# Norm sums, list indices and list masks: a PSUM operand for small VectorE operations in a four-layer graph-attention stack

## The chip, the cores and the metric

The kernel runs on one core of one Trainium2 chip. The metric is the device time of a whole execution in microseconds, as the median of several runs. Profiles come from one execution each; their times are counted from the first instruction. Engines are named as in the profile: PE (TensorE), PEld (its weight loads), DVE (VectorE), ACT (ScalarE), POOL (GpSimd), and SP (SyncE), which here only issues DMAs.

## The reference

The input x has 8 batches of 2048 rows of 64 features; adj is a 2048 x 2048 matrix of zeros and ones, with few ones outside its first rows. Four layers follow each other, each of the form x = x + f(relu(layernorm(x))):

```python
# layer 0: dot-product attention over the ones of adj
scores = einsum('bnd,bmd->bnm', h, h) * D ** -0.5
out = einsum('bnm,bmd->bnd', softmax(where(adj > 0, scores, -1e12)), h)
# layers 1 and 3: additive attention
h = h @ W
e = leaky_relu((h @ a1)[:, :, None] + (h @ a2)[:, None, :], 0.2)
out = elu_or_relu(softmax(where(adj > 0, e, -9e15)) @ h)
# layer 2: four dot-product heads over adj + I, a projection, one more
# dot-product attention, leaky_relu and a layernorm of the result
```

`_layernorm` subtracts the mean over the 64 features and divides by the root of the variance plus 1e-5.

## The kernel before

Since adj is sparse, the kernel turns it into lists and gathers rows by them. The 8 batches lie beside each other, so a row is 8 x 64 = 512 numbers (F = 512, B = 8), and the 2048 rows are 16 tiles of 128 partitions. For each tile, `lists` (from L620 on) multiplies a tile of adj by a falling key, takes the largest keys with MAX8 and MATCH_REPLACE8 on DVE (L632 to L644), and writes row numbers into `idx` (L652 for the first K entries of each row, L707 for the T packed ones, which hold the entries beyond K of the few long rows) and masks for padding into `mba` and `mbb` (L654, L708). `qidx` (L704) is the like for a query table. `ROWS`, `PACKED` and `WIDTH` set K, T and the number of keys for each tile; together the 16 tiles have 81 slots, and 26 gathered slots fit into SBUF at a time (`RING`).

Six stages follow each other in time, held apart by tables in DRAM that have to be complete before rows can be gathered from them:

1. norm of the input, 16 row tiles, into table 0, and the mean of all rows (L363, L375)
2. lists, gathers from table 0, scores, weighting, layer 0's result, its norm, table 1
3. additive attention of layer 1, its norm, table 2 and the query table
4. layer 2's four heads, table 3
5. layer 2's last attention, its own norm and the next layer's, table 4
6. additive attention of layer 3, output

Gathers (L259) are indirect DMAs, one for each slot, issued by POOL. POOL also weights rows (L389, L782), sums rows for the mean row (`acc`, L368) and takes the power -0.5 in the norms (L299). SP issues all other DMAs in a queue of its own: tiles of adj (L619), rows of x and of the tables (L268), stores of rows (L363), of x (L489) and of the mean row (L375).

The norm has two parts, written as stages of a software pipeline: `norm_a` sums a tile's rows (L276); then either it takes minus the mean (L288) and has ACT square x with that as a bias, eight times, one for each batch (L290), or it takes the mean (L280), subtracts it (L283) and has ACT square the difference (L284). `norm_b` sums the squares (L296), makes variance plus epsilon of it (L297), and POOL takes the power (L299) and, in the first form, multiplies by minus the mean (L301). `scaled` lets ACT apply it, in eight instructions again (L307). Stages 1 and 3 use the first form, 2 and 5 the second; stage 5 has two norms for each tile.

`tiny` hands out pieces of one PSUM tile of 128 x 512, `bank[0]`, in turn and from the start again when the end is reached. A new such tile is made for stages 1 and 2, for 3, and for 5 and 6. Before the change it holds the mean of L280, and copies of weights and scores that DVE reads (L541, L556, L880); all of these are written and read by DVE alone. The results of L276, L288, L296 and L297 lie in SBUF, and so do both operands of L652, L654, L707 and L708.

`pipeline` calls its stages for tile n, n-1, n-2 and so on in one step, the last stage first. The source order isn't the order of execution: when the program is built, a scheduler with cost estimates of its own writes each engine's queue, within the dependencies that it sees between tiles. Each engine then works through its queue in order. A change in the operands can therefore move instructions on all engines.

Of the kernel before, what the change touches and what calls it, by code (L numbers as in the profile page):

```python
# [8 lines left out]
F32 = mybir.dt.float32  # L9
# [4 lines left out]
OP = mybir.AluOpType  # L14
AX = mybir.AxisListType

P = 128
NEG = -1.0e30
SLOPE = 0.2
EPS = 1e-5  # L20
# [16 lines left out]
QE = 4  # L37

SPREAD = 3


MAKING = [15, 14, 13, 0, 12, 11, 10, 1, 9, 2, 8, 3, 7, 4, 6, 5]
# [19 lines left out]
def edge_stack(ctx: ExitStack, tc: tile.TileContext, x_in, adj, w1, w1t, a1, wh, wht, bh, wo, bo,  # L62
# [9 lines left out]
    nc = tc.nc  # L72
    N, F = x_in.shape
    D = gamma.shape[0]
    B = F // D
    NT = N // P
    H = bh.shape[0] // D
    INV_D = 1.0 / D
# [6 lines left out]
    small = ctx.enter_context(tc.tile_pool(name="small", bufs=4))  # L85
# [8 lines left out]
    idx = const.tile([P, NS], I32, name="idx")  # L94
    mba = const.tile([P, NS], F32, name="mba")
# [111 lines left out]
    def heads(t, n=B):  # L207
        return t.rearrange("p (b d) -> p b d", b=n)

    def wide(t, n=B):  # L210
        return t[:, :, None].to_broadcast([P, n, D])
# [15 lines left out]
    bank, spot, rows_pool, more_pool, own_pool, thin = [None], [0], [None], [None], [None], [None]  # L227
    kept = {}

    def tiny(n):  # L230

        at = spot[0] if spot[0] + n <= F else 0
        spot[0] = at + n
        return bank[0][:, at:at + n]

# [16 lines left out]
    def gather(k, i, st, behind=None):  # L252

        n = SLOTS[i]
        assert sum(SLOTS[j] for j in held) + n <= RING
        held[i], front[0] = front[0], (front[0] + n) % RING
        cols = table[k].shape[1]
        for t in range(n):
            g = nc.gpsimd.indirect_dma_start(  # L259
                out=ring[:, (held[i] + t) % RING, :cols], out_offset=None, in_=table[k][:, :],  # L260
                in_offset=bass.IndirectOffsetOnAxis(ap=idx[:, OFF[i] + t:OFF[i] + t + 1], axis=0))
            if behind is not None and t == 0:
                tc.add_manual_dep(g.ins, behind.ins.name, mybir.DependencyInfo(
                    mybir.DependencyClass.Sync, mybir.DependencyReason.DATA), reason="gather")
# [7 lines left out]

    def norm_a(src, st, centre):

        s = small.tile([P, B], F32, name="ln_s")
        nc.vector.tensor_reduce(s, heads(src), AX.X, OP.add)  # L276
        st["sq"] = rows_pool[0].tile([P, F], F32, name="ln_sq", bufs=4)
        if centre:
            mean = tiny(B)
            nc.vector.tensor_scalar(mean, s, INV_D, None, op0=OP.mult)  # L280
            st["less"] = None
            st["src"] = rows_pool[0].tile([P, F], F32, name="ln_xc", bufs=3)
            nc.vector.tensor_tensor(heads(st["src"]), heads(src), wide(mean), op=OP.subtract)  # L283
            nc.scalar.activation(st["sq"], st["src"], AF.Square)  # L284
            return
        st["src"] = src
        st["less"] = small.tile([P, B], F32, name="ln_m")
        nc.vector.tensor_scalar(st["less"], s, -INV_D, None, op0=OP.mult)  # L288
        for b in range(B):
            nc.scalar.activation(st["sq"][:, b * D:(b + 1) * D], src[:, b * D:(b + 1) * D], AF.Square,  # L290
                                 bias=st["less"][:, b:b + 1])

    def norm_b(st):

        q = small.tile([P, B], F32, name="ln_q")
        nc.vector.tensor_reduce(q, heads(st["sq"]), AX.X, OP.add)  # L296
        nc.vector.tensor_scalar(q, q, INV_D, EPS, op0=OP.mult, op1=OP.add)  # L297
        st["rstd"] = small.tile([P, 2, B], F32, name="ln_r")
        nc.gpsimd.tensor_tensor(st["rstd"][:, 0, :], q, mhalf, op=OP.pow)  # L299
        if st["less"] is not None:  # L300
            nc.gpsimd.tensor_tensor(st["rstd"][:, 1, :], st["less"], st["rstd"][:, 0, :], op=OP.mult)  # L301
# [17 lines left out]
    def pre_b(i, st):  # L319
        norm_b(st)  # L320
# [165 lines left out]
    def add_store(i, st, p, centre, more=0.0):  # L486
        x = st["x"]
        nc.vector.scalar_tensor_tensor(x, p, more, x, op0=OP.add, op1=OP.add)
        nc.sync.dma_start(out=xs[i], in_=x)  # L489
        norm_a(x, st, centre)  # L490
# [24 lines left out]
    def additive(k, wd, *finish):  # L515
        def take(i, st):
            n = order.index(i)
            gather(k, i, st, taken[k, order[n - SPREAD]] if n >= SPREAD else None)

# [14 lines left out]
        def first(i, st):  # L534
            K, T = ROWS[i], PACKED[i]
            w = slots(w_all, i)
            s = slots(s_all, i)
            n = 2 * B if k == 4 else B
            fs = f1s[:, i].rearrange("p t b -> p (t b)")[:, :n]
            pr = tiny(2 * B)  # L540
            nc.vector.tensor_copy(pr[:, :n], fs)  # L541
            pv = by_edge(i, fs, n)
            for t, m, g in rows(i, 0, K):
                nc.vector.tensor_tensor(s[:, t:t + m, :], g[:, :, F:], pr[:, None, :B].to_broadcast([P, m, B]),
                                        op=OP.add)
            for t, m, g in rows(i, K, K + T):
                nc.vector.tensor_tensor(s[:, t:t + m, :], g[:, :, F:], pv[:, t - K:t - K + m, :B], op=OP.add)
            taken[k, i] = leaky(s, s)
            if k == 4:
                nc.vector.tensor_tensor(s[:, :K, :], s[:, :K, :], pr[:, None, B:].to_broadcast([P, K, B]),  # L550
                                        op=OP.subtract)
                nc.vector.tensor_tensor(s[:, K:, :], s[:, K:, :], pv[:, :, B:], op=OP.subtract)
                nc.vector.tensor_scalar(s, s, 60.0, None, op0=OP.min)
            nc.scalar.activation(w, s, AF.Exp)  # L554
            wp = tiny((K + T) * B)
            nc.vector.tensor_copy(wp, w.rearrange("p t b -> p (t b)"))  # L556
            st["wp"] = wp.rearrange("p (t b) -> p t b", b=B)
# [31 lines left out]
    with tc.tile_pool(name="rows", bufs=2) as rp:  # L589
        rows_pool[0] = rp  # L590
        sel_all[0] = rp.tile([P, sum(PACKED) * P], F32, name="sel", bufs=1)
        with tc.tile_pool(name="lists", bufs=2) as pool, \
# [14 lines left out]
            pe = pool.tile([P, NT], F32, name="pe", bufs=1)  # L607
            nc.gpsimd.iota(pe, pattern=[[P, NT]], base=0, channel_multiplier=1,
                           allow_small_or_imprecise_dtypes=True)
            nn = pool.tile([P, NT], F32, name="nn", bufs=1)  # L610
            nc.vector.tensor_scalar(nn, pe, -1.0, N + 1.0, op0=OP.mult, op1=OP.add)
            tri = pool.tile([P, P], F32, name="tri", bufs=1)
# [8 lines left out]
            def lists(i, st):  # L621

                K, T, W = ROWS[i], PACKED[i], WIDTH[i]
# [15 lines left out]
                ell = small.tile([P, W + 2], F32, name=f"ell{W}", bufs=2)  # L639
# [9 lines left out]
                at = OFF[i]  # L649
                me = nn[:, i:i + 1]  # L650
                nc.scalar.copy(ell[:, W + 1:W + 2], me)
                nc.vector.tensor_scalar(idx[:, at:at + K], ell[:, :K], -1.0, N + 1.0, op0=OP.mult, op1=OP.add)  # L652
                if K > 1:
                    nc.vector.tensor_scalar(mba[:, at + 1:at + K], ell[:, 1:K], 0.0, NEG, op0=OP.is_equal, op1=OP.mult)  # L654
                st8 = small.tile([P, 8], F32, name="st8")
                deg, half, nmid = st8[:, 0:1], st8[:, 1:2], st8[:, 2:3]
                junk = small.tile([P, W], F32, name=f"junk{W}", bufs=1)
# [15 lines left out]
                for e0 in range(0, E, LS):  # L673
                    n = min(LS, E - e0)
# [5 lines left out]
                for t0 in range(0, T, 4):  # L680
                    n = min(4, T - t0)
# [5 lines left out]
                ke = small.tile([P, max(PACKED)], F32, name="ke")[:, :T]  # L687
                V = W - K
                step = min(T, F // (V + 2))
                mp = mbb[:, at + K:at + K + T]  # L690
                for t0 in range(0, T, step):
                    n = min(step, T - t0)
# [6 lines left out]
                    for t in range(n):  # L699
                        eq = pool.tile([P, P], F32, name="eq")  # L700
                        nc.vector.scalar_tensor_tensor(eq[:, :V], iotaj[:, :V], col[:, t:t + 1], pv[:, t, :V],
                                                       op0=OP.is_equal, op1=OP.mult,
                                                       accum_out=ke[:, t0 + t:t0 + t + 1])
                    nc.vector.tensor_scalar(qidx[:, POFF[i] + t0:POFF[i] + t0 + n], pv[:, :, V + 1], -1.0, N + 1.0,  # L704
                                            op0=OP.mult, op1=OP.add)
                    nc.vector.tensor_tensor(mp[:, t0:t0 + n], ke[:, t0:t0 + n], pv[:, :, V + 1], op=OP.is_equal)
                nc.vector.tensor_scalar(idx[:, at + K:at + K + T], ke, -1.0, N + 1.0, op0=OP.mult, op1=OP.add)  # L707
                nc.vector.tensor_scalar(mp, mp, NEG, None, op0=OP.mult)  # L708

            pipeline(xin_rows, lambda i, st: norm_a(st["x"], st, False), pre_b, pre_c(None), pre_d(0, None))  # L710
            pipeline(load_adj, lists, take0, both(first0, xin_rows), second, third0, pre_b, pre_c(u1),
                     pre_d(1, u1))

# [148 lines left out]
    with psum_pools()[0] as ps_q, psum_pools()[1] as ps_t, tc.tile_pool(name="rows2", bufs=2) as rp:  # L862
# [33 lines left out]
        def third3(i, st):  # L896
            y = st["y"]
            divide(st, y)
            nc.vector.tensor_tensor(heads(y), heads(y), over_d(bo_b), op=OP.add)
            t = rows_pool[0].tile([P, F], F32, name="z2", bufs=4)  # L900
            leaky_max(t, y, rows_pool[0].tile([P, F], F32, name="att"))
            norm_a(t, st, True)
# [28 lines left out]
        v = small.tile([P, 4], F32, name="v", bufs=1)  # L931
# [520 lines left out]
```

## Time and profile before

| | us |
|---|---|
| median of 3 runs | 1659.34 |
| lowest and highest | 1657.62, 1660.49 |
| span of the profiled execution | 1660.9 |
| DVE busy | 1311.9 |
| PE busy | 1214.6 |
| POOL busy | 1151.1 |
| ACT busy | 741.6 |

The profiled execution's time is given by its span alone; nothing around it is listed. Busy times of different engines overlap, so they don't add up to the span. What counts is which engine is full in which stage, and what ends each engine's waits there. A group of instructions is shown by its source line, engine and operation, what it writes and reads, the shapes, and how many there are.

### The profile page before, as it was taken

The page shows a single profiled execution, that of the slowest core. Times are in us where ns is not written, and L with a number is a line of the kernel's source. Part 1 is how long each engine was busy: PE and PEld are TensorE (multiplying, and loading weights), DVE is VectorE, ACT ScalarE, POOL GpSimd, SP SyncE. Part 2 cuts the span into 40 slices and gives each one's busy share as a digit, 9 for nine tenths or more (in the row PEclk, how much of TensorE's full clock was granted, in tenths as well). Part 3 has the DMA queues.
Part 4 walks back from the last instruction along what each step waited for, and adds up shares of the span by engine and source line. Part 5 has one row for each costly group of instructions (what it writes and reads, how often), then busy time and mean ns, then how long its engine had stood idle before and what let it go on. Part 6 is the DMA issues. An engine that isn't in the chain of part 4 may idle for free. (4 is left out here: it accounts for less than half of the span.)

```text
span 1660.9 us, 15702 instructions
## 1 busy us (share of the span) xinstructions
PE 1214.6 (73%) x3771; PEld 606.7 (37%) x3771; DVE 1311.9 (79%) x2674; ACT 741.6 (45%) x2362; POOL 1151.1 (69%) x903
## 2 busy tenths in 40 slices
PE   0025576776789974599997999999576868846898
PEld 0012243343454541234343344443233424423555
DVE  5978999994669987799999799861179979954667
ACT  5851223443257783356632455554334445560011
POOL 5765866786764215899689889998277889656650
PEclk9998877986889997799999999999877978857899
DMA  5545554453776537656255345300273443126771
GB/s 167 181 163 179 171 191 164 140 193 125 213 256 231 183 157 271 233 180 222 92 202 184 123 142 188 138 13 13 102 259 121 146 127 114 64 77 198 228 213 63
DMA packets 85787, 266.94 MB, mean 161 GB/s; under 512 B 14627, under 2 KB 14659, under 8 KB 75446
## 3 DMA queue, kind: packets, MB, share of 16 engines
q0 software_dynamic: 37328, 141.05, 27.4%
q1 hardware_dynamic: 48358, 124.79, 21.0%
q8 instruction: 32, 0.52, 0.1%
q14 instruction: 69, 0.57, 0.1%
HBM read 208.74 MB, written 57.05 MB: 160 GB/s over the span
## 5 line engine op out<-in xcount | busy, mean ns | idle before, releaser
L259 POOL DMA_INDIRECT g<-table,idx x405 | 396.2, 978 | 222.4 <-issue 131.7
L782 POOL TENSOR_TENSOR wh<-g,w 128x1024 f32<-128x1024 f32 x162 | 307.3, 1917 | 30.0 <-PE y L797 27.9
L394 PE MATMUL y<-wg,ident 128*128 128x512 f32 x392 | 232.4, 720 | 74.4 <-POOL wg L389 67.8
L299 POOL TENSOR_TENSOR ln_r<-ln_q,mhalf 128x8 f32<-128x8 f32 x80 | 135.9, 1702 | 129.0 <-DVE ln_q L297 93.0
L769 DVE TENSOR_REDUCE s<-prod 128x32 f32<-128x2048 f32 x81 | 183.9, 2285 | 14.6 <-ACT w L771 14.4
L389 POOL TENSOR_TENSOR wg<-g,w 128x1024 f32<-128x1024 f32 (+1 forms) x91 | 160.0, 1767 | 39.7 <-ACT w L445 31.7
L797 PE MATMUL y<-wh,ident 128*128 128x512 f32 x320 | 154.3, 609 | 28.1 <-POOL wh L795 24.4
L394 PE MATMUL y<-wg,selt 128*128 128x512 f32 x256 | 142.7, 669 | 6.0 <-POOL wg L389 6.0
L394 PEld LDWEIGHTS y<-wg,ident 128*128 128x128 f32 x392 | 79.6, 223 | 160.4 <-POOL wg L389 82.8
L797 PE MATMUL y<-wh,selt 128*128 128x512 f32 x256 | 124.6, 613 | 10.4 <-POOL wh L782 10.4
L805 ACT ACTIVATE yn<-y,rec 128x64 f32<-128x64 f32 x512 | 110.7, 366 | 27.6 <-PE y L797 26.8
L765 DVE TENSOR_TENSOR prod<-q,g 128x2048 f32<-128x2048 f32 x49 | 111.4, 2274 | 5.2 <-ACT g L763 5.1
L389 DVE TENSOR_TENSOR wg<-g,tiny 128x1024 f32<-128x1024 f32 (+1 forms) x92 | 98.1, 1086 | 12.3 <-PE y L394 11.9
L451 DVE SCALAR_TENSOR_TENSOR zt<-m,bhc,att 128x512 f32<-128x512 f32 x64 | 47.2, 737 | 74.9 <-ACT att L450 74.8
L408 PE MATMUL m<-w,selt 128*128 128x8 f32 (+1 forms) x384 | 61.0, 262 | 54.0 <-ACT w L554 19.1
L408 PEld LDWEIGHTS m<-w,selt 128*128 128x128 f32 x384 | 63.7, 215 | 100.0 <-ACT w L554 26.6
L307 ACT ACTIVATE xh<-x,ln_r 128x64 f32<-128x64 f32 x256 | 88.2, 427 | 25.5 <-POOL ln_r L301 25.4
L797 PEld LDWEIGHTS y<-wh,ident 128*128 128x128 f32 x320 | 58.9, 193 | 104.1 <-issue 64.4
L763 ACT COPY g<-g 128x512 f32<-128x512 f32 x81 | 50.4, 622 | 98.6 <-DVE prod L765 92.6
L437 PE MATMUL q<-rows,sel 128*128 128x512 f32 x128 | 81.4, 739 | 15.4 <-DVE prod L431 8.0
L765 DVE TENSOR_TENSOR prod<-qe,g 128x2048 f32<-128x2048 f32 x32 | 73.0, 2281 | 15.6 <-DMA qe<-qtab,qidx 14.5
L315 PE MATMUL q<-ident,xh 128*128 128x128 f32 x192 | 51.3, 341 | 44.9 <-ACT xh L307 43.1
(208 smaller groups left out, 2593.9 us busy)
## 6 DMA issues: line engine op xcount, KB each, us to landing
qtab<-q SPq DMA_DIRECT2D x16, 1040.0 KB, 4.0
a<-in_adj_dram SPq DMA_DIRECT2D x16, 1024.0 KB, 7.2
q<-qtab SPq DMA_DIRECT2D x14, 1040.0 KB, 5.3
table<-xh SPq DMA_DIRECT2D x48, 256.0 KB, 2.0
rows<-table SPq DMA_DIRECT2D x48, 256.0 KB, 3.8
xs<-x SPq DMA_DIRECT2D x48, 256.0 KB, 2.1
x<-xs SPq DMA_DIRECT2D x48, 256.0 KB, 3.6
table<-xh SPq DMA_DIRECT2D x32, 260.0 KB, 2.4
```

The source lines that it names most:

```text
L259: g = nc.gpsimd.indirect_dma_start(out=ring[:, (held[i] + t) % RING, :cols], out_offset=None, in_=table[k][:, :], in_offset=bass.IndirectO ...
L299: nc.gpsimd.tensor_tensor(st["rstd"][:, 0, :], q, mhalf, op=OP.pow)
L307: nc.scalar.activation(dst[:, b * D:(b + 1) * D], st["src"][:, b * D:(b + 1) * D], func, bias=0.0 if st["less"] is None else r[:, 1, b:b + ...
L389: eng.tensor_tensor(wg[:, :m].rearrange("p t (b d) -> p t b d", b=B), g[:, :, :F].rearrange("p t (b d) -> p t b d", b=B), w[:, t0:t0 + m, ...
L394: nc.tensor.matmul(y, lhs(i, t), wg[:, t - t0, :], start=(t == 0 and own is None), stop=(t == n - 1))
L408: nc.tensor.matmul(p[:, :cols], selt(i, t), packed[:, t, :], start=(t == 0), stop=(t == T - 1))
L437: nc.tensor.matmul(qe, sel(i, t - K), q, start=True, stop=True)
L765: nc.vector.tensor_tensor(pr.rearrange("p (b h) d -> p b h d", h=H), q[:, :B * H * D].rearrange("p (b h d) -> p b h d", h=H, d=D), heads(g ...
L769: nc.vector.tensor_reduce(s[:, t - lo, :], pr, AX.X, OP.add)
L782: nc.gpsimd.tensor_tensor(wg, heads(row(i, t))[:, :, None, :].to_broadcast([P, B, 2, D]), w[:, :, 2 * k:2 * k + 2, None].to_broadcast([P, ...
L797: nc.tensor.matmul(st["ys"][j], lhs(i, t), wg[:, 4 * j:4 * j + 4], start=False, stop=(t == n - 1))
L805: nc.scalar.activation(yn[:, b, h, :], st["ys"][j][:, b, h, :], AF.Copy, scale=st["rec"][:, 4 * j + b, 2 * k + h:2 * k + h + 1])
```

## The change

Four things get an operand in the PSUM tile. In `norm_a` the sum goes into a piece of it (for both forms), and in `norm_b` the sum of squares; the operation on each then reads PSUM. The last 20 columns of the tile are set aside (`TINY` = 492) and hold two constants in the first two stages, ten columns each: N + 1 and NEG. The index operations of the lists become a subtraction from the first constant, the mask operations a product with the second; each reads one operand from SBUF and one from PSUM. The numbers computed are the same. The line numbers in the texts are those of the kernel before.

```diff
+TINY = 492
...
     def tiny(n):
-        at = spot[0] if spot[0] + n <= F else 0
+        at = spot[0] if spot[0] + n <= TINY else 0
         spot[0] = at + n
         return bank[0][:, at:at + n]
...
     def norm_a(src, st, centre):
-        s = small.tile([P, B], F32, name="ln_s")
+        s = tiny(B)
         nc.vector.tensor_reduce(s, heads(src), AX.X, OP.add)
...
     def norm_b(st):
-        q = small.tile([P, B], F32, name="ln_q")
-        nc.vector.tensor_reduce(q, heads(st["sq"]), AX.X, OP.add)
-        nc.vector.tensor_scalar(q, q, INV_D, EPS, op0=OP.mult, op1=OP.add)
+        q, v = small.tile([P, B], F32, name="ln_q"), tiny(B)
+        nc.vector.tensor_reduce(v, heads(st["sq"]), AX.X, OP.add)
+        nc.vector.tensor_scalar(q, v, INV_D, EPS, op0=OP.mult, op1=OP.add)
...
+            beyond, never = bank[0][:, TINY:TINY + 10], bank[0][:, TINY + 10:]
+            nc.vector.memset(beyond, N + 1.0)
+            nc.vector.memset(never, NEG)
...
-                nc.vector.tensor_scalar(idx[:, at:at + K], ell[:, :K], -1.0, N + 1.0, op0=OP.mult, op1=OP.add)
+                nc.vector.tensor_tensor(idx[:, at:at + K], beyond[:, :K], ell[:, :K], op=OP.subtract)
                 if K > 1:
-                    nc.vector.tensor_scalar(mba[:, at + 1:at + K], ell[:, 1:K], 0.0, NEG, op0=OP.is_equal, op1=OP.mult)
+                    nc.vector.scalar_tensor_tensor(mba[:, at + 1:at + K], ell[:, 1:K], 0.0, never[:, 1:K],
+                                                   op0=OP.is_equal, op1=OP.mult)
...
-                nc.vector.tensor_scalar(idx[:, at + K:at + K + T], ke, -1.0, N + 1.0, op0=OP.mult, op1=OP.add)
-                nc.vector.tensor_scalar(mp, mp, NEG, None, op0=OP.mult)
+                nc.vector.tensor_tensor(idx[:, at + K:at + K + T], beyond[:, :T], ke, op=OP.subtract)
+                nc.vector.tensor_tensor(mp, mp, never[:, :T], op=OP.mult)
```

## The prediction

> **What bounds the kernel now.** I read the busy shares first, then cut the span into stages, then looked at single groups of instructions.
>
> ```profile
> PE 1214.6 (73%) x3771; PEld 606.7 (37%) x3771; DVE 1311.9 (79%) x2674; ACT 741.6 (45%) x2362; POOL 1151.1 (69%) x903
> ...
> DVE  5978999994669987799999799861179979954667
> ACT  5851223443257783356632455554334445560011
> ```
>
> DVE is the busiest engine, and slices 4 to 9 hold it at nine tenths. The stages are separated by row tables that have to be complete before the next stage can gather from them. Their ends are read from the stores of the mean row (L375: the first at 108.7 us, the last at 1499.8) and from the timeline. In this table of stretches each row gives PE, PEld, DVE, ACT and POOL busy.
>
> ```profile
> 0.00:109.00 109.00, 5.88 (x16) 3.50 (x16) 83.22 (x279) 75.95 (x265) 68.31 (x83) 1.00 0.50 162
> 109.00:392.00 283.00, 186.85 (x582) 97.88 (x582) 266.79 (x820) 95.40 (x332) 209.78 (x156) 0.86 0.53 174
> ...
> 1235.00:1500.00 265.00, 191.52 (x534) 97.27 (x532) 224.18 (x449) 133.74 (x445) 194.21 (x143) 0.77 0.34 109
> ```
>
> Stage 1 (to 109) has two nearly full engines: from 18.3 to 104.7 us DVE is busy 77.7 and ACT 75.7 of 86.4. Stage 2 (109 to 392, lists and first attention) is DVE's: 266.8 of 283, 16 idle. Stage 5 (1235 to 1500) has DVE at 224 of 265. The chain that ended last begins at 1548 us, where the change does nothing, so it doesn't help here.
>
> Now the small operations the change touches. Columns: count, total us and mean ns, idle before; the two lines with slashes give min/median/max ns.
>
> ```profile
> L297 DVE TENSOR_SCALAR ln_q<-ln_q 128x8 f32<-128x8 f32 x80 | 25.3, 316 | 0.3
> ...
> L280 DVE TENSOR_SCALAR tiny<-ln_s 128x8 f32<-128x8 f32 x48 | 7.6, 158 | 0.1
> ...
> L707 DVE TENSOR_SCALAR idx<-ke 128x2 int32<-128x2 f32 x5 | 4.6, 912 | 0.0
> ...
> L704 DVE TENSOR_SCALAR qidx<-m 128x2 int32<-128x2 f32 x5 | 0.8, 152 | 0.0
> ...
> L297 DVE TENSOR_SCALAR ln_q<-ln_q x80: 147/162/2566, 22.9 to 1488.9; 128x8 f32<-128x8 f32 x80
> ...
> L280 DVE TENSOR_SCALAR tiny<-ln_s x48: 143/157/171, 159.3 to 1486.0; 128x8 f32<-128x8 f32 x48
> ```
>
> The same shape with both operands in SBUF takes up to 2566 ns, and with one in PSUM never more than 171. The excess is waiting for POOL, as the timeline shows (start, length):
>
> ```profile
> 51.78 1.29 POOL L368 TENSOR_TENSOR acc<-acc,xh 128x512 f32<-128x512 f32 x1 [2.78 <-ACT xh L307]
> 51.84 1.25 DVE L288 TENSOR_SCALAR ln_m<-ln_s 128x8 f32<-128x8 f32 x1
> ...
> 19.65 7.75 ACT L290 ACTIVATE ln_sq<-x,ln_m 128x64 f32<-128x64 f32 x32
> 28.39 5.41 ACT L307 ACTIVATE xh<-x,ln_r 128x64 f32<-128x64 f32 x16 [0.73 <-POOL ln_r L301]
> ```
>
> A 0.16 us operation that starts under a POOL operation ends with it. (A bracket holds the idle time before and what ended it.) The last two lines price ACT for later: eight squares 1.94 us, eight scalings 2.71, together 4.65 us for one row tile.
>
> [...] The trace shows no such difference (157 against 162 ns); I take zero.
>
> **The change, part by part.**
>
> *What is removed: the blocking.* Busy time of a line in a stage less its count times its undisturbed median. Stage 1: L288 6.98 - 16 x 0.164 = 4.4, L297 0.5. Stage 2: L297 6.72 - 15 x 0.162 = 4.3; L652 7.35 - 13 x 0.156 = 5.3; L654 6.29 - 11 x 0.152 = 4.6; L707 9.00 - 16 x 0.152 = 6.6; L708 3.32 - 16 x 0.144 = 1.0; sum 21.8. Stage 3: nothing (17 of L297 in 2.79, 16 of L288 in 2.50). Stage 5: 12.68 - 32 x 0.162 = 7.5. In all 34 us of DVE time.
>
> *What is added.* Two memsets before the first row arrives, hidden by the wait for x until 16.8 us. 174 operations read PSUM: 0 by the rows above[...]. The reduces into PSUM (L276, L296) cost nothing: a 2048-wide reduce takes 2285 ns into PSUM (L769) and 2282 into SBUF (L344). POOL's wait for the result is unchanged, since q stays in SBUF.
>
> *What is moved.* All small values share one PSUM tile. In the order of the built program before, L276 of five row tiles stands ahead of the first L296; in that of the change, every writer and reader of the tile stands on DVE exactly as the source calls them, though their columns are disjoint. So in stage 1 the sum of tile i+1 stands behind q of tile i, and q of tile i needs ACT's squares of tile i. The index and mask operations of the lists read the constants there, so they stand behind the last of the 16 norms. The trace of before can't show this wait; the built order does, and I price it with the durations above.
>
> DVE's queue in stage 1 becomes: nine norms mixed with all the list work that can be done ahead of the first index, then seven norms with nothing between. The first part holds what DVE does before 102 us now, 79.3, less the 4.9 of blocking, less six and a half norms at 1.42 (two reduces at 0.6, two small at 0.1, start to start) = 9.2, less 0.4 for the six list operations that fall behind: 65 us. To that come waits: 2.0 for x, 4.0 for the first squares (no other sum may run meanwhile), and about 5.7 for three adjacency loads, which SP now issues behind a row store and its reload or behind a freed buffer (L619 lands in 7.2 us). From 14.6 us this ends at 91. Then six periods of ACT's 4.65 plus two handovers, 4.75 each: 28.5, the last L296 at 120. Here DVE idles about 20 us, and nobody else can use it. From the last L296 to the mean row's store now takes 108.7 - 97.5 = 11.2; about 10.5 then, so 130. Stage 1: +21. Lower end +10, if the scheduler's first part runs without the load waits and ACT keeps up; upper end +28. I use +20. SP's row stores and POOL's acc move with the tiles; their counts stay.
>
> Stage 2: all 21.8 us could be gained, since DVE is the bound and POOL has 73 us left. But L652 to L708 of tile n+4 now stand behind the norm of tile n, so the lists, which ran seven tiles ahead at the first norm, run four ahead, and less work is there to fill a wait for a gather or for y. I take 60%: -13, between -22 and +5. Stage 3: no blocking; sums and variances join the chain that the copied weights of L556 were in already. +2, between 0 and +8. Stage 5: half of 7.5 would be gained (DVE has 40 us idle there), while two variances a step join the chain: -1, between -7 and +8. Stages 4 and 6: DVE's order is the same in 4 and nearly so in 6, 0.
>
> Sum: 20 - 13 + 2 - 1 = +8. The profiled span is 1660.9, no separate outer time being shown; it lies 1.6 above the median of the three runs, 1659.3. On that median: 1667 us.
>
> **The rivals.**
> - *The released port wins.* Place: stage 2, on DVE. Price: -22 there and -7 in stage 5, with stage 1 only +10: -19, 1640 us. It decides as soon as the first stage's delay is less than what stages 2 and 5 return. For it: DVE 94% busy in stage 2. Against: 20 us of idle DVE in stage 1 that is fixed by the order.
> - *The chain locks stages 2 and 5 too.* +20, 0 in stage 2 as stalls eat the gain, +8 and +8: +36, 1695. For it: DVE is in order, and an index operation at its head waits for PE, which waits for POOL (L394 waits 92 us for wg).
> - *The PSUM form is blocked as well*[...]: then stage 2 gives nothing back, +22, 1681. Against it: 171 ns at most for L280.
> - *Gain and loss cancel*, within 3.3 us.
>
> **How the numbers follow.** 0.2%, 3.3 us, is about what a measurement of this kernel can tell from no change. The likeliest case (1663 to 1680) gets 0.45, the two dearer ones 0.25 together: slower 0.70. Cancelled 0.10. The released port 0.20, faster. The range leaves out the far end of both sides: 1643 to 1690; the likeliest case's own is 1663 to 1680.
>
> **What would show it.** Right: the first L375 near 130 us instead of 108.7; between about 91 and 120 us DVE idle before L296 with ACT's squares as releaser, ACT full; L297, L652, L654, L707 and L708 all near 150 ns with a maximum under 250; stage 2 shorter than 283 by 5 to 20. Wrong: first L375 before 115 (no lock), or maxima still over 1 us (no release), or a stage 2 longer than 283 (the lock rules there).

## The result, and the profile after

The changed kernel is **slower**: 1724.88 us (median of 4 runs, 1722.53 to 1727.07) against 1659.91 us (4 runs), ratio 1.0379, 95% interval 1.0356 to 1.0403. The profiled execution has a span of 1723.5 us, 62.6 more than the one before.

Lines 40 to 600 of before stand one line lower now (L277 is the sum, L297 and L298 the variance, L300 the power); L571 is stage 3's projection, L580 and L581 the ELU's exponentials, L582 the ELU itself; L652, L654, L707 and L708 have become L656, L658, L712 and L713. First the page after, its parts 1 and 2:

```profile
PE 1222.6 (71%) x3771; PEld 610.1 (35%) x3771; DVE 1296.9 (75%) x2676; ACT 744.1 (43%) x2362; POOL 1146.5 (67%) x903
...
DVE  5938998884468997599999699861179778963576
ACT  3581232444265775155633355555334434551101
```

DVE has 15 us *less* to do (1311.9 before), and the span is 63 us longer. So time was lost in waits. The third slice of DVE's row, a 7 before, is a 3 (from 86 to 129 us), while ACT shows 8 there, a 5 before. Now the stretches of the stages (PE, PEld, DVE, ACT and POOL busy), after, and then stages 2 and 5 of before:

```profile
0.00:127.30 127.30, 5.84 (x16) 3.50 (x16) 79.66 (x274) 76.28 (x264) 62.55 (x83) 1.00 0.43 138
127.30:422.00 294.70, 202.46 (x612) 110.82 (x612) 250.96 (x831) 99.21 (x348) 214.86 (x158) 0.76 0.52 170
422.00:679.20 257.20, 190.53 (x672) 101.44 (x672) 189.25 (x366) 145.80 (x399) 110.10 (x116) 0.90 0.56 187
...
1230.00:1559.10 329.10, 212.32 (x581) 104.23 (x580) 248.64 (x493) 144.72 (x466) 227.06 (x175) 0.78 0.40 128
```

```profile
108.70:402.60 293.90, 195.84 (x612) 103.96 (x612) 268.58 (x826) 99.61 (x348) 213.75 (x158) 0.84 0.52 170
...
1190.20:1499.80 309.60, 213.19 (x580) 108.42 (x580) 246.41 (x493) 143.09 (x466) 226.98 (x175) 0.75 0.41 136
```

The ends of the stages are the mean row's three stores, ACT's first copy of a gathered row in layer 2 (L763 before) and the last copy into table 3's rows (L854 before). The same ends before are 108.7, 402.6, 639.6, 1190.2 and 1499.8 us. By difference:

| stage | before | after | change |
|---|---|---|---|
| 1 | 108.7 | 127.3 | +18.6 |
| 2 | 293.9 | 294.7 | +0.8 |
| 3 | 237.0 | 257.2 | +20.2 |
| 4 | 550.6 | 550.8 | +0.2 |
| 5 | 309.6 | 329.1 | +19.5 |
| 6 | 161.1 | 164.4 | +3.3 |

The prediction's stretches for stages 2 and 5 were cut elsewhere (to 392 us, and from 1235 us), so its 283 us for stage 2 can't be set against the 294.7 here. Between the same two events the stage is 0.8 us longer.

The release itself took place; that what DVE and POOL share there is a port, as the rival's name has it, was my assumption, and no run shows it. Each row is one line's instructions: count, min/median/max in ns, first and last start.

```profile
L298 DVE TENSOR_SCALAR ln_q<-tiny x80: 145/157/167, 21.9 to 1549.5; 128x8 f32<-128x8 f32 x80
...
L658 DVE SCALAR_TENSOR_TENSOR mba<-ell,tiny x14: 141/146/149, 117.2 to 370.8; 128x2 f32<-128x2 f32 x6, 128x1 f32<-128x1 f32 x5, 128x8 f32<-128x8 f32 x1, 128x5 f32<-128x5 f32 x1
...
L713 DVE TENSOR_TENSOR mbb<-mbb,tiny x16: 105/144/158, 130.1 to 381.0; 128x1 f32<-128x1 f32 x8, 128x2 f32<-128x2 f32 x5, 128x3 f32<-128x3 f32 x2, 128x8 f32<-128x8 f32 x1
```

In the variance and the four list lines (L298, L656, L658, L712, L713) the maxima are 149 to 167 ns where they were 1175 to 3930. Reading PSUM made the variance no slower (157 ns at the median, 162 before). Three operations take a little longer: the mean, which now has both operands in PSUM, 174 ns where it took 157, and the two 512-wide sums, which now go to PSUM, 686 to 695 where they took 674 to 676. That is less than 3 us of DVE in all. Stage 2 has 250.96 us of DVE work where it had 268.58, and is as long as before: 43.7 us of DVE's idle time instead of 25.3.

Stage 1 lost its time as the prediction said. The waits of DVE up to 127.3 us (total, times, longest), and DVE's timeline (start, length, and in brackets the idle time before and what ended it):

```profile
DVE tiny L297 <- ACT ln_sq L291: 21.1, 8, 3.4
```

```profile
102.63 0.69 DVE L297 TENSOR_REDUCE tiny<-ln_sq 128x8 f32<-128x512 f32 x1 [2.66 <-ACT ln_sq L291]
103.36 0.17 DVE L298 TENSOR_SCALAR ln_q<-tiny 128x8 f32<-128x8 f32 x1
103.56 0.69 DVE L277 TENSOR_REDUCE tiny<-x 128x8 f32<-128x512 f32 x1
...
107.19 0.69 DVE L297 TENSOR_REDUCE tiny<-ln_sq 128x8 f32<-128x512 f32 x1 [2.66 <-ACT ln_sq L291]
```

The reader sees the lock: DVE forms one variance, the next tile's sum and its mean, and waits 2.66 us, once every 4.56 us, which is ACT's time for one tile. The wait for squares was 0.5 us in this stage before and is 21.1 now. ACT is full meanwhile (the fourth busy time of this row):

```profile
91.00:120.00 29.00, 0.00 (x0) 0.00 (x0) 9.60 (x24) 27.92 (x98) 19.84 (x20) 1.00 0.35 112
```

Stage 3 holds a wait that I hadn't foreseen at all. The timeline after, DVE first, then POOL, ACT and PE:

```profile
457.29 0.17 DVE L298 TENSOR_SCALAR ln_q<-tiny 128x8 f32<-128x8 f32 x1
...
458.31 0.20 DVE L476 RECIPROCAL seen<-seen 128x8 f32<-128x8 f32 x1
482.37 0.70 DVE L582 SCALAR_TENSOR_TENSOR q<-q,e 128x512 f32<-128x512 f32 x1 [23.86 <-ACT e L581]
...
483.83 0.69 DVE L277 TENSOR_REDUCE tiny<-x 128x8 f32<-128x512 f32 x1
...
466.72 0.95 POOL L260 DMA_INDIRECT g<-table,idx  x1 [0.30 <-issue]
467.69 1.67 POOL L300 TENSOR_TENSOR ln_r<-ln_q,mhalf 128x8 f32<-128x8 f32 x1
...
473.09 1.67 POOL L300 TENSOR_TENSOR ln_r<-ln_q,mhalf 128x8 f32<-128x8 f32 x1
474.74 0.35 POOL L302 TENSOR_TENSOR ln_r<-ln_m,ln_r 128x8 f32<-128x8 f32 x2
...
474.97 5.41 ACT L308 ACTIVATE xh<-x,ln_r 128x64 f32<-128x64 f32 x16 [17.74 <-POOL ln_r L302]
...
475.80 0.48 PE L316 MATMUL q<-ident,xh 128*128 128x128 f32 x1 [17.76 <-ACT xh L308]
```

Read it backwards. DVE stands still from 458.5 to 482.4 us with the ELU (L582) at its head. Behind it comes the sum of that tile (L277), and every other piece of the small bank, such as the copies of scores and weights for the next tiles, stands behind that sum, so DVE's queue has nothing to put ahead. That this order is the reason is an inference here; the run late_s below bears it out. The ELU waits for ACT's exponentials, these for PE's projection, PE for ACT's scaled rows, ACT for POOL's powers. The variances for those were ready at 452.1 and 457.5 us, but POOL's queue has gathers ahead, one every 1.25 us, until 467.7. DVE, ACT and PE stand still together for more than 16 us. In the kernel before, DVE waited for these exponentials five times, 1.1 us at most:

```profile
DVE q L581 <- ACT e L580: 2.7, 5, 1.1
```

In stage 5 two waits of DVE have grown, for y and for rows that ACT scales (q). After:

```profile
DVE y L481 <- PE y L395: 13.8, 6, 4.9
DVE q L912 <- ACT q L308: 12.1, 5, 5.2
```

and before:

```profile
DVE y L480 <- PE y L394: 8.8, 4, 4.3
...
DVE q L907 <- ACT q L307: 3.5, 2, 3.3
```

There is no single stall. These two make 13.6 us of the 17.3 by which DVE's idle time grew in the stage.

### The profile page after: what moved, and what is told of

It is laid out like the page before. It is cut to its first block, busy times and chain, and to the rows that moved or that the text cites. A ratio compares the mean times of both kernels' runs of the same rounds, so it can differ in the third digit from the quotient of the medians.

```text
span 1723.5 us, 15766 instructions
## 1 busy us (share of the span) xinstructions
PE 1222.6 (71%) x3771; PEld 610.1 (35%) x3771; DVE 1296.9 (75%) x2676; ACT 744.1 (43%) x2362; POOL 1146.5 (67%) x903
## 5 line engine op out<-in xcount | busy, mean ns | idle before, releaser
L395 PE MATMUL y<-wg,ident 128*128 128x512 f32 x392 | 239.1, 742 | 84.5 <-POOL wg L390 70.2
L300 POOL TENSOR_TENSOR ln_r<-ln_q,mhalf 128x8 f32<-128x8 f32 x80 | 132.4, 1656 | 153.2 <-DVE ln_q L298 109.8
L390 DVE TENSOR_TENSOR wg<-g,tiny 128x1024 f32<-128x1024 f32 (+1 forms) x92 | 98.0, 1086 | 12.3 <-PE y L395 12.2
L308 ACT ACTIVATE xh<-ln_xc,ln_r 128x64 f32<-128x64 f32 x256 | 65.1, 335 | 50.5 <-POOL ln_r L300 50.4
L369 POOL TENSOR_TENSOR acc<-acc,xh 128x512 f32<-128x512 f32 x45 | 60.3, 1339 | 39.5 <-ACT xh L308 36.9
```

The lines of the kernel that those rows point to most:

```text
L308: nc.scalar.activation(dst[:, b * D:(b + 1) * D], st["src"][:, b * D:(b + 1) * D], func, bias=0.0 if st["less"] is None else r[:, 1, b:b + ...
L390: eng.tensor_tensor(wg[:, :m].rearrange("p t (b d) -> p t b d", b=B), g[:, :, :F].rearrange("p t (b d) -> p t b d", b=B), w[:, t0:t0 + m, ...
L395: nc.tensor.matmul(y, lhs(i, t), wg[:, t - t0, :], start=(t == 0 and own is None), stop=(t == n - 1))
```

## The experiments

Three theories. **A**: the loss is the order in which the pieces of the small bank have to be written and read. **B**: PSUM as an operand costs. **C**: any disturbance makes the scheduler write other queues, and those of before are better than what it usually finds. The runs fall into four groups, each with its own runs of the kernel before. In two of them (order_only, two_src, norms, lists; order_pinned, free_pinned, neutral, loose), which ran on two other chips, that kernel took 1706 to 1708 us instead of 1661 or 1662. So ratios are against the same group's runs, and stages 3 to 6 of those eight are compared with free_pinned, whose queues and operands there are those of before. Each stage's time comes from one profile, and the sum of a row misses the change of the median time by up to 5 us (neutral: 6.9 against 11.6), late_v's, whose profile is of its slowest run, by 8. So single entries of 5 us and less tell little.

The table has the change of each stage in us (the kernels are described below it): for stages 1 and 2 against before_again (110.9 and 293.5), for 3 to 6 against before_again (234.5, 550.8, 308.6, 161.2) or, in those eight, free_pinned (254.4, 551.5, 314.2, 183.6).

| kernel | 1 | 2 | 3 | 4 | 5 | 6 | ratio (95%) |
|---|---|---|---|---|---|---|---|
| before_again | 0 | 0 | 0 | 0 | 0 | 0 | 1.0004 (0.9992 to 1.0017) |
| after_again | +18.2 | +4.2 | +21.9 | +0.4 | +21.2 | +0.9 | 1.0363 (1.0345 to 1.038) |
| order_only | +16.5 | +12.1 | +23.5 | +0.6 | +24.0 | +0.9 | 1.044 (1.0397 to 1.0483) |
| order_pinned | +17.0 | +8.2 | +18.9 | 0 | +28.2 | +0.5 | 1.0422 (1.0371 to 1.0474) |
| norms | +17.1 | -6.8 | +19.2 | +1.6 | +21.6 | +3.3 | 1.0324 (1.0301 to 1.0347) |
| early | +17.0 | +5.3 | +11.6 | +1.1 | +9.6 | -1.4 | 1.0259 (1.0242 to 1.0277) |
| early_pinned | +16.4 | -0.2 | +2.8 | +0.9 | +2.4 | +1.5 | 1.0145 (1.0119 to 1.017) |
| late | -1.9 | -4.3 | +19.1 | +0.5 | +21.2 | +0.8 | 1.0236 (1.0219 to 1.0253) |
| late_s | -2.7 | -0.5 | +24.0 | +2.1 | +3.8 | +2.3 | 1.0189 (1.0162 to 1.0216) |
| late_v | -2.3 | +1.8 | +12.4 | +24.5 | +26.9 | +1.9 | 1.0338 (1.0313 to 1.0363) |
| lists | -3.4 | -5.5 | +13.1 | 0 | +10.2 | +0.4 | 1.0112 (1.009 to 1.0133) |
| two_src | -8.6 | +16.5 | +18.8 | -1.0 | +7.5 | -1.0 | 1.0218 (1.0174 to 1.0263) |
| neutral | -0.8 | +9.7 | +1.2 | -0.3 | -2.7 | -0.2 | 1.0072 (1.0044 to 1.0099) |
| loose | -4.9 | -8.3 | +12.2 | +1.7 | -0.5 | +0.8 | 1.0012 (0.9991 to 1.0032) |
| free_pinned | -5.8 | -7.2 | | | | | 0.9931 (0.9912 to 0.995) |
| all_free | -5.9 | -8.8 | +1.9 | +0.7 | +0.6 | -0.9 | 0.9906 (0.9881 to 0.9932) |

### The yardsticks: before_again and after_again

Edit: none.

> The kernel before, unchanged, as a yardstick: the four runs above were on a chip where it takes 1708 us. All theories: ratio 1.000. Its stages show which of the losses of stages 3 and 6 in those runs belong to the chip (all four have 182 to 187 us in stage 6, where the first profile had 161) and which to the kernels: if the chip, stage 3 here near 255 and stage 6 near 184.

> The changed kernel, unchanged, on the same chip as the line before it: ratio 1.03 to 1.045. Stage by stage against that line the differences of the first pair should return: +18.6, +0.8, +20.2, +0.2, +19.5, +3.3 us, each within 5 us if a loss belongs to the written order and not to the chip.

The stages of before return within 2.5 us, so the longer stages 3 and 6 of those eight (254.4 and 183.6 us in free_pinned) belong to their chips. The differences of the first pair return within 3.4 us, so those of 5 us and more are the kernels' own on this chip.

### The order alone: order_only and order_pinned

order_only is the kernel before with this around each operation that the change gives a piece of the bank, and around the users that it had already:

```diff
+    def turn(x):
+        if tail[0] is not None:
+            tc.add_manual_dep(x.ins, tail[0].ins.name, mybir.DependencyInfo(
+                mybir.DependencyClass.NoSync, mybir.DependencyReason.SCHED_ONLY), reason="turn")
+        tail[0] = x
+        return x
...
-        nc.vector.tensor_reduce(s, heads(src), AX.X, OP.add)
+        turn(nc.vector.tensor_reduce(s, heads(src), AX.X, OP.add))
```

order_pinned gives every instruction of the kernel before, on all five engines, its place in the changed kernel's queue (`code` holds the steps from place to place, `mine` the engine's instructions as the source calls them):

```diff
+        for step in array.array("h", zlib.decompress(base64.b85decode(code))):
+            at += step
+            if last is not None:
+                tc.add_manual_dep(mine[at], last.name, mybir.DependencyInfo(
+                    mybir.DependencyClass.NoSync, mybir.DependencyReason.SCHED_ONLY), reason="pin")
+            last = mine[at]
```

> The kernel before with its operands and places (all SBUF[...]), plus one thing: every operation that the change gives a piece of the small bank is made to follow, on DVE, the last one that has such a piece, as the source calls them. No wait is added, only a written order. Theory A (the order of the pieces is the loss): about as slow as the changed kernel or slower by the blocking, 1715 to 1755 us; mean row's first store at 125 to 132 us, stage 3 near 257 us, L297's maximum over 1 us again. Theory B (PSUM as an operand costs): 1660, mean row at 109. Theory C (the scheduler falls into another arrangement by accident): anywhere, with losses in other stages than the changed kernel's.

> The kernel before, every operation and operand as it was, but each engine's queue (all five) written in exactly the order that the changed kernel's queues have; no wait added. Order theory (the whole loss is the order of the queues): at least as slow as the changed kernel, ratio 1.036 to 1.06, the excess being the blocking[...] in stages 1 and 2 (up to 34 us of DVE time); stage 1 near 129 us, stage 3 near 256, stage 5 near 330. If PSUM operands cost something themselves: faster than the changed kernel, ratio under 1.033.

Both are as slow as the changed kernel or somewhat slower, in the same stages. In order_pinned's trace all five engines work in the order of the changed kernel's. **The order of the queues carries the whole loss**, without any change of operands; theory B falls. Whether the part of that order which the pieces impose (A) or the rest of what the scheduler wrote (C) costs the time, these two don't tell. The blocking is back, as its line in order_pinned shows:

```profile
L410 DVE TENSOR_SCALAR ln_q<-ln_q x80: 149/171/4382, 21.8 to 1587.2; 128x8 f32<-128x8 f32 x80
```

At this order the release is worth about half a per cent (1.0422 against 1.0363 and 1.0379), which the overlapping intervals leave open.

### Halves of the change: norms, lists, early, late

norms and lists each undo the other half's edits (constants and index operations; or `s` and `v` back to `small`). early switches the norms' pieces off at the start of stage 3; late has the lists of before and switches them on there (True in the last line, False ahead of it):

```diff
-        s = tiny(B)
+        s = tiny(B) if banked[0] else small.tile([P, B], F32, name="ln_s")
...
-        q, v = small.tile([P, B], F32, name="ln_q"), tiny(B)
+        q = small.tile([P, B], F32, name="ln_q")
+        v = tiny(B) if banked[0] else q
...
             order[:] = ORDER1
+            banked[0] = False
```

> The change for the norms alone (sum and variance in the small bank), lists as before. Theory A: nearly the whole loss, since the norms' own order sets stages 1, 3 and 5: 1710 to 1745 us, mean row at 122 to 130. Lists' blocking (L652 to L708) back to means over 300 ns. Theory B: about half the loss, 1690.

> The change for the lists alone (constants in the small bank), norms as before. Theory A: no lock in stage 1 (the mean of a centred norm is the only other user there, from stage 2 on): mean row at 106 to 112, stage 2 shorter by 5 to 20 us, 1640 to 1660 in all. Theory B: 1690. Theory C: anything between 1640 and 1720.

> The changed kernel, but from stage 3 on the norms' sums and variances are in SBUF again as before; stages 1 and 2 as changed. Theory A: +19 in stage 1, about 0 in stages 2 to 6: ratio 1.008 to 1.016. Theory C (the scheduler's arrangement by accident): stages 3 and 5 may lose although no order is imposed there, ratio up to 1.035.

> The other half: stages 1 and 2 as in the kernel before, from stage 3 on the norms' sums and variances in the small bank. Theory A: 0 in stages 1 and 2, +20 in stage 3, +20 in stage 5: ratio 1.02 to 1.028. Theory C: stages 3 and 5 lose another amount, since what they start from differs; ratio 0.995 to 1.035.

norms has nearly the whole loss. lists keeps stage 1 and gains 5.5 in stage 2, as A expects, but loses 13.1 and 10.2 in stages 3 and 5, where none of its edits is but the narrower ring of pieces (`TINY`). early does the same (+11.6, +9.6). These two were against theory A alone: stages with no new order lose a half to two thirds of what the changed kernel loses there. late came as A expects.

Stage 2 shows something that the halves hide. Each half alone shortens it (norms by 6.8 and lists by 5.5 us, on one profile each), by about what each takes off DVE there (6.5 and 6.1 of 268.4 us). Together they take 17 us off DVE and shorten nothing. Only together do the lists' operations stand behind the norms' sums and variances, which is the loss that the prediction saw for this stage; no run isolates it.

### Is it the arrangement? neutral, two_src, early_pinned

neutral adds 16 operations that no one reads; two_src takes the constants from SBUF tiles as a second source; early_pinned is early with the queues of stages 3 to 6 in the order of before, written as in order_pinned.

```diff
# neutral
                 st8 = small.tile([P, 8], F32, name="st8")
+                nc.vector.memset(st8[:, 7:8], 0.0)
# two_src
-        nc.vector.tensor_scalar(q, q, INV_D, EPS, op0=OP.mult, op1=OP.add)
+        nc.vector.scalar_tensor_tensor(q, q, INV_D, tiny_eps, op0=OP.mult, op1=OP.add)
...
-        nc.vector.tensor_scalar(st["less"], s, -INV_D, None, op0=OP.mult)
+        nc.vector.tensor_tensor(st["less"], s, minus_d, op=OP.mult)
```

> The kernel before with one column of an unread scratch tile set to zero in each of the 16 lists: 16 operations of about 0.1 us on DVE, under 2 us of work, no order, no PSUM. It only makes the scheduler arrive at other times. Theory C (a good part of the loss is that any disturbance gives another arrangement of stages 3 and 5): stages 3 and 5 longer by 5 to 12 us each, ratio 1.006 to 1.016. If the arrangement does not matter: 1.000 to 1.002.

> The kernel before, with the same operations[...]: the constant comes from a small SBUF tile as a second source, no PSUM, no shared tile. Theory A: release without the order: first mean row at 105 to 112 us, L297, L652, L654, L707, L708 with maxima under 250 ns, 1630 to 1660 us. If a second SBUF source doesn't release the port: maxima over 1 us and 1660. Theory C: a new arrangement, 1640 to 1720, with no stage that must suffer.

> The line called early (stages 1 and 2 as changed, norms in SBUF from stage 3 on), with the queues of stages 3 to 6 written in the order of the kernel before; stages 1 and 2 stay as the scheduler wrote them there. Theory C for the 9 + 9 us that early lost in stages 3 and 5: they go, ratio 1.010 to 1.016 in place of 1.026. If they come from something carried over from stage 2 (a late ring of rows, a late load): they stay, 1.022 to 1.027.

early_pinned settles it: with the old queues (from stage 3 on its trace has the order of before on all five engines), early's 11.6 and 9.6 us shrink to 2.8 and 2.4. So those losses were **the scheduler's other arrangement**, theory C. neutral suggests how little it takes: with 16 operations of 59 ns, 0.9 us of work, the kernel is 0.72% slower, and in its trace all five engines work in another order than before, while before_again's order is the same throughout. The old queues weren't tried with neutral, so the arrangement is the likely cause and not a shown one. My expectation had the place wrong, since stages 3 and 5 were spared and stage 2 lost 9.7.

two_src missed its main aim, though its first stage came out 8.6 us shorter. A second source in SBUF didn't release DVE here (the lines of the variance and of minus the mean):

```profile
L300 DVE SCALAR_TENSOR_TENSOR ln_q<-ln_q,fixed_n x80: 143/158/1879, 22.5 to 1548.1; 128x8 f32<-128x8 f32 x80
...
L291 DVE TENSOR_TENSOR ln_m<-ln_s,fixed_n x32: 141/158/943, 17.9 to 667.4; 128x8 f32<-128x8 f32 x32
```

The variance, 0.16 us at the median, took up to 1.88 us, and minus the mean up to 0.94. That it was POOL that held them, as it did in the timeline of before, is inferred from these maxima. The run's loss of 18.8 us in stage 3 is again one without an imposed order.

### Which piece locks which stage: late_s and late_v

late with only the sums, or only the variances, in the bank:

```diff
# late_s
-        v = tiny(B) if banked[0] else q
+        v = q
# late_v
-        s = tiny(B) if banked[0] else small.tile([P, B], F32, name="ln_s")
+        s = small.tile([P, B], F32, name="ln_s")
```

> The line called late (stages 1 and 2 as before, from stage 3 on the norms in the small bank) with the sums alone in the bank, variances in SBUF. If the sum is what locks stage 3 (it can only be formed behind the ELU, and the copies of f and of the weights for the next tiles are queued behind it): the single wait of 24 us of DVE's L581-line for ACT's e is there, stage 3 at +15 to +20. Stage 5: if the variance is what locks there, +0 to +9, ratio 1.010 to 1.018 in all.

> The same with the variances alone in the bank, sums in SBUF. If the sum locks stage 3: no single wait over 10 us there, stage 3 at +0 to +13 (the accidental part). If the variance locks stage 5 (DVE may not form it early or late, and so waits for ACT's scaled rows): +15 to +22 there; ratio 1.010 to 1.020 in all.

DVE's waits for ACT's e (ELU, stage 3) and for ACT's scaled rows q (stage 5), of late_s:

```profile
DVE q L584 <- ACT e L583: 25.5, 3, 22.8
...
DVE q L911 <- ACT q L310: 3.1, 2, 2.9
```

of late_v:

```profile
DVE q L911 <- ACT q L310: 15.4, 4, 5.2
...
DVE q L584 <- ACT e L583: 13.6, 2, 12.6
```

and of early_pinned, where no norm is in the bank in these stages:

```profile
DVE q L677 <- ACT e L676: 2.5, 5, 1.1
```

The sum brings the one long wait of stage 3 (22.8 us in late_s, 23.7 in late, 23.9 after), and alone costs nothing much in stage 5 (+3.8). The variance brings the waits of stage 5 (+26.9). The split isn't clean: late_v has a wait of 12.6 us in stage 3 too, which I had excluded, and loses 24.5 us in stage 4, where neither kernel has a piece of the bank. DVE waits there once for 20.2 us for ACT's weights, for which it waits 10.0 us at most in before_again. I count that to C, but no run isolates it; it lifts the ratio above the range given. In the stages aimed at, both runs came out above their ranges too: late_s with +24.0 in stage 3, late_v with +26.9 in stage 5.

### The release without the order: loose, free_pinned, all_free

In these three the operands are those of the change, and DVE's operations on pieces in different columns are declared independent (`keep` holds the earlier users of the same columns, whose order stays):

```diff
+    def touch(x, *spans):
...
+        for y in keep:
+            tc.add_manual_dep(x.ins, y.name, mybir.DependencyInfo(
+                mybir.DependencyClass.NoSync, mybir.DependencyReason.DATA), reason="piece")
+        tc.declare_no_dep(x.ins, group=group, keep=keep, query=mybir.DependencyQuery.ANY,
+                          reason="other columns")
...
-        nc.vector.tensor_reduce(v, heads(st["sq"]), AX.X, OP.add)
+        touch(nc.vector.tensor_reduce(v, heads(st["sq"]), AX.X, OP.add), at)
```

loose does this in stages 1 and 2 (the norms of four tiles of 32 there, and all from stage 3 on, have their values in SBUF) and leaves the queues to the scheduler. free_pinned writes them in the order of before besides, but for one neighbouring pair on DVE. all_free does it in all stages, exactly in the order of before, with the norms' pieces in 128 columns of their own.

> The operands of the line before the last (stages 1 and 2 as changed, order among pieces lifted, norms from stage 3 on in SBUF), but the queues left to the scheduler. Theory A alone: as that line, 0.983 to 0.997. With theory C: its gain in stages 1 and 2, then the accidental losses of stages 3 and 5 seen in the line called early (+9 each): ratio 0.997 to 1.010.

> The mirror image: all five queues in exactly the order of the kernel before, but in stages 1 and 2 the operands of the change (sums and variances of 28 of the 32 norms there, constants of all lists, in the small bank), with the order among pieces in different columns lifted. Release theory: L297, L652, L654, L707, L708 under 250 ns at most, stage 1 at 104 to 109 us and stage 2 shorter by 5 to 22 us, stages 3 to 6 unchanged within 3: ratio 0.983 to 0.997, faster than both kernels. If the release is worth nothing at a fixed order: 0.998 to 1.002.

> All five queues in exactly the order of the kernel before, all the operands of the change in all stages (sums and variances of 76 of 80 norms, constants of all lists), with the norms' pieces in columns of their own and the order among pieces lifted. Release theory: as free_pinned in stages 1 and 2 (-6, -7 us), and in stage 5 a part of the 7.5 us of blocking there: -1 to -6; ratio 0.987 to 0.993. If stage 5's blocking is covered by its idle time: 0.992 to 0.994.

free_pinned and all_free are **faster than both kernels**, all_free by 0.94% against before, 1647.24 us where that took 1662.48. Its stretches, rows 1, 2 and 5:

```profile
0.00:105.00 105.00, 5.89 (x16) 3.51 (x16) 78.98 (x279) 75.56 (x264) 68.37 (x83) 1.00 0.51 168
105.00:389.70 284.70, 192.73 (x612) 101.48 (x612) 249.78 (x826) 99.06 (x348) 213.76 (x158) 0.83 0.52 176
...
1177.60:1486.80 309.20, 217.23 (x580) 110.57 (x580) 241.40 (x493) 142.85 (x466) 226.80 (x175) 0.73 0.42 136
```

DVE has 18.8 us less to do in stage 2 than before (268.58), and the stage is 9 us shorter: half of what is released reaches the end. In stage 5 it has 5.0 us less (246.41 before), and the stage isn't shorter, which fits with blocking that lay beside DVE's idle time. So the ratio falls into the range given for a gain in stage 5, but the gain lies in stages 1 and 2. loose keeps the gain of stages 1 and 2 and loses it again in stage 3, as C expects, though only there.

## Why the prediction was wrong, point by point

The kernel lost 62.6 us where I had forecast +8. Stages 3 and 5 lost 39.7 of them, and I had put those two at +1 together: the price of the chain there is the step that failed. Stage 2's gain, put at -13, is missing as well.

- **What bounds the kernel, and stage 1: right.** DVE waits for ACT's squares in a fixed order, ACT is full (27.92 us of the 29.00 from 91 to 120), the first mean row comes at 127.3 where I had 130 by the working and +20 as the value taken. Measured +18.6 and +18.2; +16.4 to +17.1 in every other kernel that has the norms' order there, none in those that don't.
- **The release: right that it comes**, with maxima of 149 to 167 ns where I had named 250 as the most. Its worth was mis-sized only a little: at a fixed order it is 15 us (all_free), where the working took some 22 (4.9 in stage 1, 13 in stage 2, half of 7.5 in stage 5) of the 34 us of blocking counted.
- **The price of PSUM: right, by a wrong reading.** L280, on which I set it at zero, wrote PSUM and read SBUF, so it couldn't test a PSUM source (L704, shown beside it, did read PSUM, at 152 ns). L298 does, and it shows no price (157 ns at the median against 162). Nor does DVE's next operation start later at the order of before: 76 ns behind the variance's start at the median in all_free, 80 in before_again. (In the changed kernel's order the sum L277 follows 17 times, 190 to 210 ns behind that start, where L276 before followed 3 times, 60 to 70 ns behind it; what sets this apart was not shown.) That the sums into PSUM cost nothing was nearly right, they take 10 to 20 ns more each.
- **Stage 2, -13, measured +0.8 and +4.2: the term was mis-sized.** I took 60% of 21.8 us for what is left of the gain when lists run less far ahead. At the order of before the gain is 7 to 9 us, and the order costs 8 to 12 (order_pinned, order_only). The gain was near half and the loss as large. The result lies inside my bounds (up to +5), but the sign that I had named for being right, a shorter stage 2, did not come.
- **Stage 3, +2 with 8 as the upper end, measured +20.2: the step failed.** I reasoned that the copies of weights were in the chain already, so that little would be added. But the sum can only be formed behind the ELU at the end of a tile, and all later copies then stand behind it: late_s has the wait of 22.8 us with the sum as the only addition.
- **Stage 5, -1 with 8 as the upper end, measured +19.5: the step failed.** Two variances a tile seem to fix the place of all pieces of both norms. I saw that they join the chain and put it at some 3 us without a reason. late_v shows +26.9, late +21.2, and late_s, without the variances, +3.8. And the 7.5 us of blocking that I had returned by half return nothing (all_free, +0.6).
- **The rivals.** "The chain locks stages 2 and 5 too" (1695 us) was the right kind; its +8 for stage 3 and for stage 5, the dear ends of those two steps, were each less than half of what was measured. My upper end, 1690, lay even below that rival's price. "The PSUM form is blocked as well" is refuted by the 167 ns above. "The released port wins" had stage 1 at +10 and needed the full release in stages 2 and 5; a gain came only with the order lifted (all_free, -15 us, where that rival had -19).
- **What no step had:** that the scheduler's queues of before are better as a whole than what it wrote after the edits tried here, though single stages also came out shorter (two_src, stage 1, -8.6). In stage 3, kernels without an imposed order lost 1.2, 11.6, 12.2, 13.1 and 18.8 us. How much of the changed kernel's 20 there is the forced wait and how much the arrangement, stays open: with the sums' order it was 18.9 to 24.0, so the two aren't a sum. In stage 5 they stand apart: -2.7 to +10.2 without the variance's order, +19.5 to +28.2 with it.

## What to carry to other kernels

A small tile that is shared by pieces was one object for the scheduler here, so putting a value there ordered it against all others. Count for each new piece what it must wait for and who stands behind it in the engine's queue, in every stage, above all where it comes at the end of a tile's work. Price an edit under an automatic scheduler in two parts, the operation at the old order and the new order itself, and measure them apart by writing the old queues down; the one edit here that was meant to be harmless came to 1.007. About half of the blocked time of the busy engine (9 of 18.8 us) came back in stage 2 when it was released, and none of 5.0 us in stage 5, where that engine had 63 us of idle time.

## What the runs showed of the hardware that was not expected

The variance, an operation of 8 elements a row, took up to 1879 ns with two SBUF sources (two_src), 2566 with one (before), and never more than 167 with a PSUM source (80 of them, after). The one of 2566 ns ended at 204.21 us, and the POOL operation beside it (L389) at 204.16; for the one of 1879 no view shows what POOL did. One held operation did not get in between two of POOL's: the longest of L707 before, 3.93 us from 176.60, began under one POOL operation (to 178.08), lasted through the next (178.04 to 178.64), and ended at 180.53 with the third, which ended at 180.50. At the same order, the PSUM operands took 27.8 us of DVE's busy time away (1311.9 to 1284.1) and 15 us of the kernel's. Beside that, and not a matter of the hardware alone: sixteen VectorE operations of 59 ns, whose result nobody reads, came with 0.72% (0.44 to 0.99) of the kernel's time, with all five queues written differently around them.
